# A decoder layer with 64 experts: weights packed and requested by pairs, the last norm's additions on VectorE

## The chip, the cores and the metric

The kernel runs on one core of a Trainium2 chip. The metric is the device time of one execution in microseconds (us). The core's engines are TensorE (PE, its weight loads PEld), VectorE (DVE), ScalarE (ACT), GpSimd (POOL) and SyncE (SP), which here only issues transfers. Each engine works through its own instructions in order and waits on semaphores for the others. Sixteen DMA engines serve every queue.

## The reference

All is float32. `x` has 32 batches of 256 tokens of width 256, the context has 32 batches of 120 tokens. Three stages follow each other, each with a residual and a layer norm:

```python
x = layernorm(x + self_attention(x))          # 16 heads of 16, rotary q and k
x = layernorm(x + cross_attention(x, ctx))    # 16 heads, two softmaxes of 8 dims each, a1 - lam * a2
x = layernorm(x + ffn(x))

# ffn: 64 experts, top 6 of them for each token, at most 96 tokens an expert
scores = sigmoid(x @ router_weight.T)
_, top_idx = top_k(scores + expert_bias, 6)
probs = top_scores / sum(top_scores)
y = gelu(xs @ w1[e]) @ w2[e]                   # xs: the 96 slots of expert e, 256 -> 128 -> 256
out[token] += probs * y
out += gelu(x @ sw1.T) @ sw2.T                 # the shared expert, 256 -> 512 -> 256
```

## The kernel before

**Order of the work.** Every engine is wrapped in `InOrder` (lines 162 to 190): its call is at line 172, so nearly every row of the profile carries L172, and it ties each instruction to the one before it on its engine. So the order in which the Python code calls `pe`, `dve`, `act`, `pool` and `sp` is the order on those engines. Buffers are given out by a scheduler: `tile(..., tag=..., bufs=n)` takes one of n slots of that tag that its readers have left, whichever it is; a name of its own with `bufs=1` takes always the same slot.

**Stage one, the attentions (lines 282 to 1008).** Each batch has a list of steps (lines 398 to 491), written by hand as (tick, part, function). A tick runs, in this order, the parts "pre", the score matmuls of the batches in their score phases together with what reads them (`maxima`: a maximum on VectorE into `pad_mx`; `weights`: an exponential on ScalarE into `pt`), then "av", "mm" and "post". A batch starts 16 ticks after the one before, so several are under way, and ticks that agree modulo 16 run together: tick 62 of one batch with tick 14 and tick -2 of later ones. The steps that matter here:

- `xback(0)` and `xback(1)` (ticks 60 and 61, line 818) turn the cross-attention's result into four PSUM banks of the tag "tr" (four slots in all, `bank()` at line 196). `xweigh(i)` (line 828) reads two of them on VectorE: for each softmax a reciprocal, two products into `rd` and `parts`, and then GpSimd takes the difference into `at`.
- `values` (tick 14, "av", line 743) is the self-attention's product with v. It takes a slot of "tr" too, tile `av`.
- `bias_x` (line 616) adds the output bias to the residual `xt` on GpSimd.
- `store` (line 964) writes the normed tokens to DRAM three times: transposed into `x2T_d`, as the start of the sum `acc[0]`, and zeros into `acc[1]`.
- `dispatch` (line 948) scatters each token's row, with its 64 probabilities and a code of the token (321 numbers), to its experts' places in `slots`.

**The shared expert (`shared`, lines 205 to 276)** is a generator that yields after each piece of TensorE work, 65 pieces: for each block of 512 tokens two pieces `h` (matmuls into a bank of `scp`, then a GELU into `gT`), two pieces for the block before (into a bank "tr", then a copy into `ys`). What a piece leaves for ScalarE (`before`) is called at the start of the next piece. `load` reads a block of `x2T_d` into one of three buffers.

**Stage two, the experts and the last norm (lines 1011 to 1233).** One loop over slots. `n = slot - START` counts pairs of experts: pair n is turned by TensorE (`turn`), pair n-1 does its first product (`up`), n-2 its second (`down`), and `scatter` of pair n-3 weighs the result on VectorE into `ye` and adds it to DRAM with one indirect DMA of GpSimd for each of the two experts, the first to `acc[0]`, the second to `acc[1]`. Weights and rows are requested by SP for groups of four experts: `rows_of`, `expert_weights` (a `w1t` of 512 B rows, a `w2t` of 1 KB rows), three groups ahead, through `fetch_for` in every second slot. `four` has ten buffers of 4 KB per partition, which serve the weights and later the last norm's tiles. In two of three slots up to END a piece of the shared expert is run, after that two in each slot.

From slot END on, each slot has also a step of the last norm for blocks of 512 tokens (class `Last`, lines 1121 to 1168): `fetch` (SP reads the two sums), `add` (GpSimd adds them), `stats` (VectorE adds the result to `ys` and takes mean and variance), `scale` (GpSimd: variance plus epsilon, the power -1/2, the offset in two instructions), `put` (ScalarE normalises four times 256 columns; SP writes `out`). A step calls `add` for block s, `stats` and `scale` for block s-1 and `put` for block s-2.

Of the kernel before, what the change touches and what calls it, by code (L numbers as in the profile page):

```python
# [11 lines left out]
F32 = mybir.dt.float32  # L12
# [24 lines left out]
def tile_decoder_layer(  # L37
# [18 lines left out]
    w1: bass.AP,  # L56
    w2: bass.AP,
# [8 lines left out]
    NT = B * T  # L66
    assert T == 2 * P and S <= P
# [8 lines left out]
    x2T_d = dram.tile([D, NT], F32, name="x2T_d")  # L76
# [123 lines left out]
    TB = min(512, NT)  # L200
# [4 lines left out]
    def shared(ypool):  # L205


        def load(k):
            t = ffn.tile([P, D // P, TB], F32, tag="x2T", name="x2T", bufs=3)
            sp.dma_start(  # L210
                out=t,
                in_=x2T_d[:, k * TB : (k + 1) * TB].rearrange("(c p) t -> p c t", p=P),
            )
            return t
# [17 lines left out]
        loaded = {k: load(k) for k in range(2)}  # L232
        gTs = {}
        for k in range(NBLK + 1):
            for f2 in range(2):
                if k == NBLK:
                    continue
                if f2 == 0 and k + 2 < NBLK:
                    loaded[k + 2] = load(k + 2)
                if before:  # L240
                    before()
                hp = scp.tile([P, 2, 512], F32, tag="sc", name="h")
                for f in range(2):
                    f0 = (2 * f2 + f) * P
                    for c in range(D // P):
                        pe.matmul(
                            hp[:, f, :TB],
                            lhsT=w_s1[:, c, f0 : f0 + P],
                            rhs=loaded[k][:, c, :],
                            start=(c == 0),  # L250
                            stop=(c == D // P - 1),
                        )
                gT = gTs[k, f2] = ffn.tile([P, 2, TB], F32, tag="gT", name="gT", bufs=4)
                before = lambda hp=hp, gT=gT: gelu(hp, gT)
                yield
# [26 lines left out]
    with ExitStack() as one:  # L282
# [101 lines left out]
        class Batch:  # L384
# [13 lines left out]
            def steps(self):  # L398
# [17 lines left out]
                    (-2, "pre", self.bias_x),  # L416
# [49 lines left out]
                    (62, "pre", self.xweigh, 1),  # L466
# [497 lines left out]
            def store(self):  # L964

                cols = slice(self.b * T, (self.b + 1) * T)
                sp.dma_start(
                    out=x2T_d[:, cols].rearrange("(c p) t -> p c t", p=P), in_=self.t["x2T"]
                )
# [41 lines left out]
    with ExitStack() as two:  # L1011

        four = two.enter_context(tc.tile_pool(name="four", bufs=10))
        wk = two.enter_context(tc.tile_pool(name="wk2", bufs=2))
        small = two.enter_context(tc.tile_pool(name="small2", bufs=3))
        ypool = two.enter_context(tc.tile_pool(name="ypool", bufs=NBLK))
        ypools.append(ypool)
        EG = 4
        START = 7

        def rows_of(eg):

            xs = wk.tile([CAP, EG, XPW], F32, tag="xs", name="xs", bufs=4)
            sp.dma_start(
                out=xs,
                in_=slots[eg * EG * CAP : (eg + 1) * EG * CAP, :].rearrange(
                    "(e s) d -> s e d", s=CAP
                ),
            )
            return xs  # L1030

        def tokens_of(eg):

            code = xs_of[eg][:, :, D + NE]
            empty = small.tile([CAP, EG], F32, tag="empty", name="empty")
            dve.tensor_scalar(empty, code, 0.0, slot_f[:CAP, :], ALU.is_equal, ALU.mult)
            token = small.tile([CAP, EG], F32, tag="token", name="token")
            dve.tensor_scalar(token, code, -1.0, float(NT), ALU.mult, ALU.add)
            idx = small.tile([CAP, EG], I32, name=f"idx{eg}", bufs=1)
            dve.tensor_add(idx, token, empty)  # L1040
            return idx

        def expert_weights(eg):
            es = slice(eg * EG, (eg + 1) * EG)
            w1t = four.tile([P, EG, D // P, F], F32, tag="four", name="w1t")
            sp.dma_start(out=w1t, in_=w1[es].rearrange("e (c p) f -> p e c f", p=P))
            w2t = four.tile([P, EG, D], F32, tag="four", name="w2t")
            sp.dma_start(out=w2t, in_=w2[es].rearrange("e p d -> p e d"))
            return w1t, w2t

        class Pair:


            def __init__(self, n):
                self.es = (2 * n, 2 * n + 1)

            def turn(self):
                self.ps = bank()[:, : 4 * CAP].rearrange("p (e c t) -> p e c t", e=2, c=2)
                for k, e in enumerate(self.es):
                    for c in range(D // P):  # L1060
                        pe.transpose(
                            self.ps[:, k, c, :],
                            xs_of[e // EG][:, e % EG, c * P : (c + 1) * P],
# [7 lines left out]
            def up(self):  # L1071
                self.ps = bank()[:, : 2 * CAP].rearrange("p (e t) -> p e t", e=2)
                for k, e in enumerate(self.es):
                    for c in range(D // P):
                        pe.matmul(
                            self.ps[:, k, :],
                            lhsT=weights_of[e // EG][0][:, e % EG, c, :],
# [9 lines left out]
            def down(self):  # L1087
                self.ps = bank()[:CAP].rearrange("p (e d) -> p e d", e=2)
                for k, e in enumerate(self.es):
# [3 lines left out]
                        rhs=weights_of[e // EG][1][:, e % EG, :],  # L1093
# [4 lines left out]
            def scatter(self):  # L1098
                ye = wk.tile([CAP, 2, D], F32, tag="ye", name="ye", bufs=6)
                for k, e in enumerate(self.es):  # L1100
# [3 lines left out]
                        xs_of[e // EG][:, e % EG, D + e : D + e + 1],  # L1104
# [6 lines left out]
                            ap=idx_of[e // EG][:, e % EG : e % EG + 1], axis=0  # L1111
# [9 lines left out]
        class Last:  # L1121
# [4 lines left out]
            def fetch(self):  # L1126
                self.sums = []
                for n in range(2):
                    a = four.tile([P, NQ, D], F32, tag="four", name=f"a{n}")
# [5 lines left out]
            def add(self):  # L1135
                pool.tensor_add(self.sums[0], self.sums[0], self.sums[1])

            def stats(self):
                y = ys[self.k]
                dve.tensor_add(y, y, self.sums[0])  # L1140
# [5 lines left out]

            def scale(self):
                rs = small.tile([P, NQ], F32, tag="rs", name="rs")
                pool.tensor_scalar(rs, self.mv[:, :, 1], LN_EPS, None, ALU.add)
                self.rstd = small.tile([P, NQ], F32, tag="rstd", name="rstd")  # L1150
                pool.tensor_tensor(self.rstd, rs, mhalf[:, :NQ], ALU.pow)
                self.off = small.tile([P, NQ], F32, tag="off", name="off")
                pool.tensor_tensor(self.off, self.mv[:, :, 0], self.rstd, ALU.mult)
                pool.tensor_scalar(self.off, self.off, -1.0, None, ALU.mult)

            def put(self):
                o = four.tile([P, NQ, D], F32, tag="four", name="o")
# [8 lines left out]
                sp.dma_start(  # L1166
# [17 lines left out]
        def fetch_for(eg):  # L1184
            if eg < NE // EG:
                xs_of[eg] = rows_of(eg)
                weights_of[eg] = expert_weights(eg)

        while more or steps < NBLK + 3:
# [8 lines left out]
            if slot == 1:  # L1198
                for eg in range(3):
                    weights_of[eg] = expert_weights(eg)  # L1200
            if slot == START - 2:
                for eg in range(3):
                    xs_of[eg] = rows_of(eg)
            if 0 <= n < NP and n % (EG // 2) == 0:
                eg = n // (EG // 2)
                idx_of[eg] = tokens_of(eg)

            if slot < START or slot < END and n % 3 < 2:
# [3 lines left out]
            if slot >= END and (steps == 0 or steps > NBLK or steps - 1 in whole):  # L1212
                for part, behind in (
                    (Last.add, 0),
                    (Last.stats, 1),
                    (Last.scale, 1),
                    (Last.put, 2),
                ):
                    if part is Last.add:
                        for k in range(0 if steps == 0 else steps + 2, min(steps + 3, NBLK)):  # L1220
                            last[k].fetch()
# [7 lines left out]
            if 0 <= n - 2 < NP:  # L1229
                pairs[n - 2].down()  # L1230
                if n % 2 == 1:
                    fetch_for((n - 2) // 2 + 3)
# [3 lines left out]
def _rotary(seq):  # L1236
# [5 lines left out]
    return [np.repeat(f(angles).astype(np.float32), 2, axis=1) for f in (np.cos, np.sin)]  # L1242

# [46 lines left out]
```

## Time and profile before

| what | us |
|---|---|
| median of 10 runs | 2003.45 |
| lowest and highest of them | 1996.02, 2006.68 |
| the profiled execution | 2004.6 |
| its span, first to last instruction | 2002.9 |

| stage (us from the span's start) | PE busy | DVE busy | ACT busy | POOL busy |
|---|---|---|---|---|
| 200 to 1400, attentions (1200 us) | 1190.9 | 866.2 | 681.8 | 766.3 |
| 1707.2 to 1772, experts (64.8 us) | 64.80 | 19.80 | 20.08 | 21.84 |
| 1772 to 1870.6, experts (98.6 us) | 88.46 | 28.73 | 20.59 | 48.15 |
| 1870.6 to 1914.6, last scatters (44.0 us) | 44.00 | 5.27 | 9.54 | 25.06 |
| 1914.6 to 1926.5 (11.9 us) | 0.43 | 8.00 | 6.95 | 11.18 |
| 1926.5 to 1990.6, last norm (64.1 us) | 64.06 | 38.20 | 42.16 | 60.10 |
| 1990.6 to 2002.9, end (12.3 us) | 0.11 | 3.31 | 8.45 | 2.55 |

A row gives the time in which each engine was busy within that stretch; an engine whose number is near the length of the stretch had hardly a pause in it. The page of the whole execution says 95% for PE, 62% for DVE, 51% for ACT and 59% for POOL, which are means over these stages. The rows that the prediction quotes are of four kinds. A row of waits names the engine and what it did next, who released it, the us in total, how often, and the longest. A row in order of time has the start, the duration, the engine, the instruction with its tiles (output <- inputs), its shapes, and in brackets how long the engine had stood idle and who released it. A row of a window has the stretch, its length, busy us (and instructions) of PE, PEld, DVE, ACT and POOL, the granted TensorE clock, the share of time in which the DMA engines were busy, and GB/s. A row of DMA issues has the tile, the queue, the kind, how many, and the us from issue to landing.

### The profile page before, as it was taken

Reading aid. Unit: us, or ns where it says so; the run is one execution under the profiler, and the core shown is the slowest. Engines: PE = TensorE matmul, PEld = TensorE weight load, DVE = VectorE, ACT = ScalarE, POOL = GpSimd, SP = SyncE. Lnnn points to the kernel's source line nnn. Section 1 sums busy time; section 2 is a strip of 40 time slices with the busy share of each in tenths; the row PEclk is TensorE's granted clock in tenths of the full one; section 3 lists DMA queues with packets and bytes.
Section 4 is the critical chain, followed back from the end, with each engine's and each line's share of the span. In section 5 each row is a group of like instructions: output and inputs, shape, how many; then the busy total and the mean of one; then the engine's idle time right before and its main releaser. Section 6 shows DMA issues by size and latency. Waiting matters only on the chain.

```text
span 2002.9 us, 43322 instructions
## 1 busy us (share of the span) xinstructions
PE 1906.0 (95%) x17800; PEld 1300.8 (65%) x17800; DVE 1244.4 (62%) x2750; ACT 1012.5 (51%) x1445; POOL 1185.5 (59%) x1191
## 2 busy tenths in 40 slices
PE   5999999999999999999999999999999888998977
PEld 3566666666666666666666666666666655776745
DVE  3366777777777777777777777777777643232155
ACT  1345555555555555555555555555555432321356
POOL 6233466666666666666666666666665446244687
PEclk8899999999999999999999999999999979998989
DMA  9100021111111111111111111111100014787495
GB/s 248 48 14 9 30 70 54 47 49 42 35 35 32 33 34 35 34 34 32 31 31 38 32 31 32 32 31 31 32 20 20 17 49 116 184 214 177 62 332 210
DMA packets 131813, 132.06 MB, mean 66 GB/s; under 512 B 32763, under 2 KB 118996, under 8 KB 131616
## 3 DMA queue, kind: packets, MB, share of 16 engines
q1 hardware_dynamic: 103408, 115.22, 18.8%
q0 software_dynamic: 25600, 13.02, 3.9%
q8 instruction: 140, 2.29, 0.4%
q10 hardware_dynamic: 2608, 1.07, 0.2%
q14 instruction: 57, 0.47, 0.1%
HBM read 74.62 MB, written 111.04 MB: 93 GB/s over the span
## 4 chain that ended last, share of the span: by engine, by line
PE 80%; DVE 8%; DMA 6%; POOL 3%; issue 2%; ACT 1%; SPq 0%; DVEq 0%; POOLq 0%; ACTq 0%
PE tr L172 38%; PE sc L172 26%; PE av L172 12%; DMA acc<-ye,idx 5%; PE h L172 3%; DVE pad_mx L172 2%; DVE parts L172 1%; POOL slots L172 1%; ACT pt L172 1%; DVE rd L172 1%; DVE rest L172 1%; DVE count L172 1%; DMA a<-acc 1%; DVE ye L172 0%; DVE sel L172 0%
## 5 line engine op out<-in xcount | busy, mean ns | idle before, releaser
L172 DVE TENSOR_REDUCE pad_mx<-sc 128x4 f32<-128x1024 f32 (+1 forms) x512 | 608.4, 1189 | 376.8 <-PE sc L172 371.4
L172 ACT ACTIVATE pt<-sc 128x1024 f32<-128x1024 f32 (+1 forms) x512 | 523.6, 1024 | 399.2 <-PE sc L172 399.0
L172 PE MATMUL sc<-qT,kT 32*128 32x256 f32 (+1 forms) x4096 | 574.4, 405 | 12.3 <-ACT pt L172 7.8
L172 PE MATMUL sc<-kT,qT 32*128 32x256 f32 (+1 forms) x4096 | 564.1, 396 | 10.6 <-ACT pt L172 5.4
L172 POOL DMA_INDIRECT slots<-xpt,slot x384 | 389.0, 1013 | 95.6 <-issue 92.3
L172 PEld LDWEIGHTS sc<-qT,kT 32*128 32x128 f32 (+1 forms) x4096 | 341.2, 184 | 127.1 <-issue 64.8
L172 PEld LDWEIGHTS sc<-kT,qT 32*128 32x128 f32 x4096 | 349.0, 185 | 94.2 <-issue 24.3
L172 POOL TENSOR_TENSOR qT<-qT,mT 128x512 f32<-128x512 f32 x128 | 163.5, 1295 | 144.5 <-ACT mT L172 144.5
L172 PE MATMUL tr<-w_qkv,xT 128*128 128x256 f32 (+1 forms) x512 | 193.6, 512 | 8.5 <-DMA xT<-in_xT 8.5
L172 POOL TENSOR_SCALAR rs<-mv 128x2 f32<-128x2 f32 (+1 forms) x80 | 30.1, 376 | 240.1 <-DVE mv L172 238.9
L172 POOL DMA_INDIRECT acc<-ye,idx x64 | 90.1, 1408 | 108.2 <-DVE ye L172 57.3
L172 ACT COPY ot<-av 128x512 f32<-128x512 f32 x192 | 112.1, 586 | 81.4 <-PE av L172 81.2
L172 PEld LDWEIGHTS tr<-w_qkv,xT 128*128 128x128 f32 x512 | 90.8, 192 | 77.5 <-issue 72.3
L172 PE MATMUL av<-pt,pad_v 128*32 128x256 f32 x2048 | 126.5, 388 | 10.2 <-DVE parts L172 10.2
L172 PE MATMUL h<-x2T,w_s 128*128 128x512 f32 x256 | 115.7, 602 | 12.2 <-DMA a<-acc 11.5
L172 PE MATMUL av<-pt,pad_xv 120*32 120x256 f32 x2048 | 126.3, 387 | 0.2
L172 POOL TENSOR_TENSOR rc<-qkb,cosr 128x512 f32<-128x512 f32 x64 | 82.5, 1290 | 74.2 <-DVE qkb L172 69.3
L172 PE MATMUL tr<-w_s,gT 128*128 128x256 f32 x512 | 117.1, 387 | 0.8 <-DVE ye L172 0.8
L172 ACT COPY kT<-tr 128x512 f32<-128x512 f32 (+1 forms) x128 | 70.3, 574 | 89.7 <-PE tr L172 89.7
L172 PEld LDWEIGHTS tr<-w_s,gT 128*128 128x128 f32 x512 | 99.6, 195 | 18.9 <-issue 3.8
L172 POOL TENSOR_TENSOR at<-parts 128x256 f32<-128x256 f32 x64 | 46.5, 726 | 108.8 <-DVE parts L172 108.8
L172 POOL TENSOR_TENSOR pad_qk<-rc,qkb 128x256 f32<-128x256 f32 x128 | 104.9, 840 | 5.0
(141 smaller groups left out, 2845.4 us busy)
## 6 DMA issues: line engine op xcount, KB each, us to landing
a<-acc SPq DMA_DIRECT2D x32, 512.0 KB, 5.9
xT<-in_xT SPq DMA_DIRECT2D x32, 256.0 KB, 6.4
xt<-in_x SPq DMA_DIRECT2D x32, 256.0 KB, 2.7
x2T_d<-T SPq DMA_DIRECT2D x32, 256.0 KB, 2.2
acc<-xpt SPq DMA_DIRECT2D x32, 256.0 KB, 2.7
acc<-zero SPq DMA_DIRECT2D x32, 256.0 KB, 3.0
x2T<-x2T_d SPq DMA_DIRECT2D x16, 512.0 KB, 7.8
w1t<-in_w SPq DMA_DIRECT2D x16, 512.0 KB, 6.2
```

The costliest lines, as they stand in the source:

```text
L172: ins = f(*args, **kwargs)
```

## The change

Six things change, in four places of the code.

1. The host packs the two weights of each expert side by side and the experts by pairs (`_pairs_of_experts`), so that one partition's row of a pair is 4 KB. `expert_weights` and `rows_of` request one pair, six pairs ahead, in every slot. The buffers of the weights (`four0` to `four9`), rows (`xs0` to `xs7`) and `ye` are taken in turn by name, each with `bufs=1`. `tokens_of` runs for every pair.
2. `x2T_d` is laid out by blocks, so that a block is read in rows of 4 KB; four buffers in place of three, and the third block is loaded at the start.
3. `xweigh(1)` goes from "pre" to "post" of tick 62, and `bias_x` from "pre" to "post" of tick -2.
4. In the last norm `add` is gone: VectorE adds both sums to `ys`. The epsilon is added on VectorE, the power stays on GpSimd, and the offset is one instruction on VectorE, in the step after. `put` comes one step later, and ScalarE issues the write of `out`. A step calls `offset` for block s-2, `put` for s-3 and `stats` for s-1.
5. Pieces of the shared expert run in three of four slots up to END in place of two of three.
6. `ys` has two buffers fewer.

```diff
@@ load, shared
-            t = ffn.tile([P, D // P, TB], F32, tag="x2T", name="x2T", bufs=3)
-            sp.dma_start(
-                out=t,
-                in_=x2T_d[:, k * TB : (k + 1) * TB].rearrange("(c p) t -> p c t", p=P),
-            )
+            t = ffn.tile([P, D // P, TB], F32, tag="x2T", name="x2T", bufs=4)
+            sp.dma_start(out=t, in_=x2T_d[k])
...
@@ steps
-                    (-2, "pre", self.bias_x),
+                    (-2, "post", self.bias_x),
...
-                    (62, "pre", self.xweigh, 1),
+                    (62, "post", self.xweigh, 1),
...
@@ stage two
-        four = two.enter_context(tc.tile_pool(name="four", bufs=10))
+        four = two.enter_context(tc.tile_pool(name="four", bufs=1))
...
-        EG = 4
+        AHEAD = 6
...
+        def next_four(shape):
+            return four.tile(shape, F32, name=f"four{next(fours) % 10}")
...
-        def expert_weights(eg):
-            es = slice(eg * EG, (eg + 1) * EG)
-            w1t = four.tile([P, EG, D // P, F], F32, tag="four", name="w1t")
-            sp.dma_start(out=w1t, in_=w1[es].rearrange("e (c p) f -> p e c f", p=P))
-            w2t = four.tile([P, EG, D], F32, tag="four", name="w2t")
-            sp.dma_start(out=w2t, in_=w2[es].rearrange("e p d -> p e d"))
-            return w1t, w2t
+        def expert_weights(n):
+            wt = next_four([P, 2, D // P * F + D])
+            sp.dma_start(out=wt, in_=w12[n])
+            return wt
...
-                ye = wk.tile([CAP, 2, D], F32, tag="ye", name="ye", bufs=6)
+                ye = wk.tile([CAP, 2, D], F32, name=f"ye{self.n % 6}", bufs=1)
...
@@ Last
-            def add(self):
-                pool.tensor_add(self.sums[0], self.sums[0], self.sums[1])
-
             def stats(self):
                 y = ys[self.k]
-                dve.tensor_add(y, y, self.sums[0])
+                for a in self.sums:
+                    dve.tensor_add(y, y, a)
...
-            def scale(self):
                 rs = small.tile([P, NQ], F32, tag="rs", name="rs")
-                pool.tensor_scalar(rs, self.mv[:, :, 1], LN_EPS, None, ALU.add)
+                dve.tensor_scalar(rs, mv[:, :, 1], LN_EPS, None, ALU.add)
                 self.rstd = small.tile([P, NQ], F32, tag="rstd", name="rstd")
                 pool.tensor_tensor(self.rstd, rs, mhalf[:, :NQ], ALU.pow)
+
+            def offset(self):
                 self.off = small.tile([P, NQ], F32, tag="off", name="off")
-                pool.tensor_tensor(self.off, self.mv[:, :, 0], self.rstd, ALU.mult)
-                pool.tensor_scalar(self.off, self.off, -1.0, None, ALU.mult)
+                dve.scalar_tensor_tensor(
+                    self.off, self.mv[:, :, 0], -1.0, self.rstd, ALU.mult, ALU.mult
+                )
...
-                sp.dma_start(
+                act.dma_start(
                     out=flat[self.rows, :].rearrange("(p q) d -> p q d", q=NQ), in_=o
                 )
...
@@ the loop
-            if slot < START or slot < END and n % 3 < 2:
+            if slot < START or slot < END and n % 4 < 3:
                 pieces_on(1)
...
+                for part, behind in ((Last.offset, 2), (Last.put, 3), (Last.stats, 1)):
...
+                fetch_for(n - 2 + AHEAD)
```

## The prediction

> **What bounds the kernel now.** I read the windows by stage first, then the waits inside each stage, then the DMA answers and the order of time at the few places where an engine stood still. From 200 to 1400 us the batches of the two attentions overlap and TensorE is busy 198 to 199 us of every 200. One wait stands out there (engine, who released it, us in total, times, longest):
>
> ```profile
> PE av L172 <- DVE parts L172: 9.8, 26, 1.2
> ```
>
> In the order of time one of these waits looks like this (start, duration, engine, what, idle before it):
>
> ```profile
> 621.80 0.42 DVE L172 TENSOR_TENSOR parts<-tr,rd 128x256 f32<-128x256 f32 x1
> 622.38 1.93 PE L172 MATMUL av<-pt,pad_v 128*32 128x256 f32 x32 [0.34 <-DVE parts L172]
> 622.98 1.15 DVE L172 TENSOR_REDUCE pad_mx<-sc 128x8 f32<-128x960 f32 x1
> ```
>
> The weighted sum of the first attention needs a PSUM bank; it gets one that the older batch's `xweigh(1)` has just read. So TensorE stops 0.34 us once in each batch, and the next maximum on VectorE stands behind the same instructions.
>
> The experts' stage begins near 1707. It has windows with the weights' traffic and without (us, busy us of PE, PEld, DVE, ACT, POOL, clock, DMA share, GB/s):
>
> ```profile
> 1676.00:1690.00 14.00, 9.22 (x35) 7.57 (x34) 5.43 (x24) 4.75 (x4) 10.70 (x11) 0.76 1.07 296
> 1753.00:1858.00 105.00, 94.86 (x478) 71.20 (x477) 31.12 (x90) 22.65 (x34) 47.79 (x34) 0.93 0.81 187
> 1858.00:1900.00 42.00, 42.00 (x176) 30.09 (x175) 5.74 (x15) 12.85 (x12) 27.06 (x20) 1.00 0.45 59
> 1908.00:1930.00 22.00, 10.50 (x37) 7.38 (x36) 13.26 (x36) 10.45 (x17) 19.42 (x17) 0.78 0.96 361
> ```
>
> ```profile
> acc<-ye,idx POOLq DMA_INDIRECT x34, 6.6
> ...
> acc<-ye,idx POOLq DMA_INDIRECT x20, 3.4
> ```
>
> The two lines are the scatters of 1753 to 1858 and of 1858 to 1910, with the median us from issue to landing. Each scatter adds to `acc`, so it waits for the one before it on the same half. With weights in flight a pair of experts takes 105/17 = 6.2 us, without them 4.1 (the issues at 1871.36 and 1875.47). TensorE finishes the experts at 1873, but the last scatter lands at E = 1904.6: **the scatters' chain bounds this stage**, not TensorE.
>
> After E the last norm runs:
>
> ```profile
> 1922.50 2.35 POOL L172 TENSOR_TENSOR a<-a,a 128x1024 f32<-128x1024 f32 x1
> 1924.88 1.23 DVE L172 TENSOR_TENSOR y<-y,a 128x1024 f32<-128x1024 f32 x1 [1.91 <-POOL a L172]
> 1924.93 1.26 POOL L172 TENSOR_SCALAR rs<-mv 128x4 f32<-128x4 f32 x1
> 1926.27 1.04 POOL L172 TENSOR_TENSOR rstd<-rs,mhalf 128x4 f32<-128x4 f32 x1
> 1927.88 2.36 POOL L172 TENSOR_TENSOR a<-a,a 128x1024 f32<-128x1024 f32 x1
> 1989.66 0.23 POOL L172 TENSOR_SCALAR rs<-mv 128x4 f32<-128x4 f32 x1
> ```
>
> A step lasts 5.4 us and GpSimd is full in it. The first additions wait 3.7 us after E for `a`, and meanwhile ScalarE stands 20.8 us before the first `o`; the GELUs behind it hold TensorE for 11.5 us. From E to the end of the span it is 2002.9 - 1904.6 = 98.3 us.
>
> **The change part by part.** The sum is made against the span of 2002.9; the profiled run took 2004.6 and the median is 2003.45, so I take the difference from the median.
>
> *A, `xweigh(1)` and `bias_x` after the tick.* The bank for `av` can no longer be the one of `xweigh(1)`, whose reader now comes later in VectorE's order. Free by then is the bank of the query transposes; ScalarE's copy of them ran from 621.05 to 621.63, and the last score matmul ended near 622.03. So the 0.34 us go: 9.8 us over 26 batches. What comes late: VectorE now does its maximum (1.16) first and the last `parts` ends near 625.0 instead of 623.06; `at` and `bias_x` follow on GpSimd (0.73 + 1.27), so its dispatches move from 625.3 to about 627. TensorE transposes `at` two ticks (6 us) after that wait, and GpSimd is free a third of the time: nothing. Bounds: 0, if another wait ends just as late, and -10. I take **-9.8**.
>
> *B, experts' requests.* A pair now brings 0.52 MB of weights in rows of 4 KB and 0.25 MB of rows, right after an older pair's `ye`; before, 1.5 MB came for two pairs. Rows of 4 KB ran at 361 GB/s (1908 to 1930), rows of 512 B and 1 KB at 296 (1676 to 1690): 0.52 x (1/296 - 1/361) = 0.3 us less DMA time per pair. The mixed queue of 1753 to 1858 moved a MB in about 3.7 us, so a burst took 5.6 us and put 2 x (6.2 - 4.1) = 4.2 us onto the scatters. The new one takes about 2.4. If its cost is in proportion, a pair takes 4.1 + 1.8 = 5.9 us; if the first 1.4 us hide under the 1.41 us in which GpSimd issues, as they seem to before, 4.1 + 1.0 = 5.1. TensorE itself needs 2.09 us a pair (starts 1859.87 to 1861.96) and 27 pieces of 3.45 us over 32 pairs instead of 24, so 5.0. Ends are 6.2 (no gain) and 5.0; I take the middle, 5.6, since both rows of landing (3.4 and 6.6) stay in the mix. The weights burden 22 pairs: 22 x 0.6 = **-13**; ends 0 and -24 (TensorE's own end, scatters landed near 1880). The three pieces moved forward fill TensorE's 10.1 us of waits for `ye`. Sixteen more requests on SP (0.3 to 0.5 us each) and 48 more index instructions (0.16 to 0.22 us) lie on queues that are two thirds idle: nothing; with that cover gone, 6 and 9 us.
>
> One rule speaks against B. The Trainium skill, "DMA: Bandwidth & Descriptors", section "Specifications", has 512 B as the smallest transfer at line rate, so packing would bring nothing; its section "Bandwidth" asks for 1 MiB per DMA, so splitting would cost. The trace's 296 against 361 GB/s disagrees with the first. By the rule B would be about 0 and the sum +1, 2004.6.
>
> *C, the last norm.* GpSimd loses the 2.35 us addition, the `rs` and both `off`. VectorE's step: two additions 2 x 1.23 and 0.06 between; four pairs of statistics 2.22 (1920.75 to 1922.97); `rs` 0.2 (0.23 on GpSimd alone). Then the power, which stays on GpSimd: 1.04 plus 0.15 for both handovers. `offset` of that block is the very next instruction on VectorE, so **VectorE waits out the power**, and the next block's additions are queued behind it. `offset` 0.2: in all 6.3 us against 5.4. The end: E + 3.7 for `a`, the second addition and the statistics of block 0, 3.4; 15 x 6.3 = 94.5; `rs`, power, offset 1.7; `put` 2.1; from the last `o` to the end 3.7 as before. Together 109.1, against 98.3: **+11**. Ends: -7, if the wait hides (15 x 1.2 less), and +14, if each step is 6.5.
>
> *D, the rest.* `put` one step later lets two more pieces run before ScalarE blocks: on the new E the 11.5 us stall of TensorE goes. But TensorE would then end near 1875 + 26 x 3.45 = 1965, some 25 us ahead of VectorE's chain, so the gain is not seen. Each `o` now takes the buffer of an `a` of a block two later, and waits for that addition: ScalarE runs at VectorE's pace. The output leaves through ScalarE's queue, 16 x 0.45 us (its issues at the start took 0.33 to 0.8), under that same pace: nothing; were ScalarE the bound, six `put` after TensorE's end are 6 x 2.6 = 16 us and 3 more, to 1984. SP loses 64.0 us of waits for `o`, but the loads behind them were three blocks ahead. `x2T` in 4 KB rows with a fourth buffer loads earlier what nobody waited for. All **0**.
>
> Sum: -9.8 - 13 + 11 = -11.8, so 2003.45 - 11.8 = **1991.6 us**.
>
> **The rivals.** *R1, slower.* VectorE's round through GpSimd's power is the bound of the last 100 us, and the experts' scatters are no faster, because each pair now meets a burst of its own and TensorE another wait in place of `parts`: +11 alone, 2014. It decides as soon as A and B bring less than 11 us together; beyond 0.2% when they bring under 7. For it: 6.3 against 5.4 is read directly; against it: 0.34 us in every batch. *R2, faster than forecast.* The smaller bursts hide and the scatters follow TensorE at 5.0: B = -24, 1980.6; for it, quiet gaps in the DMA rows (26 to 44 GB/s in some slices of 1753 to 1858). *R3, the bank stays.* The allocation still gives `av` the bank of `xweigh(1)`: then TensorE waits for the maximum and `parts`, from 622.05 to about 624.1, 2.1 us x 28 = +59 in place of -9.8: 2060. The order in which banks come free speaks against it. *R4, no difference.* The scatters stay at 6.2 us a pair, since the bytes in front of them are nearly the same (B = 0), and A and C cancel: -9.8 + 11, 2004.7; for it, a landing of 6.6 against 3.4 us, which bytes alone may set.
>
> **How the numbers follow.** About 4 us (0.2%) is what a measurement of this kernel can tell from no change. Forecast (1984 to 1999.4) 0.42; R2 0.20; within 0.2%, mostly R4, 0.14; R1 0.18; R3 0.06. Faster 0.62, same 0.14, slower 0.24. The forecast's own range is 1984 to 1999; the range reaches into R2 and R1, 1976 to 2011.
>
> **What would show it.** Right: TensorE no longer waits for `parts`; pairs of scatters 5.0 to 5.9 us apart with weights in flight; the two `y` additions 6.3 us from block to block, VectorE idle about 1.2 us before each `off`, released by the power; TensorE ending some 20 us before VectorE. Wrong: steps near 5.1 us (C falls to -7 and the time to the 1970s), scatters still 6.2 us a pair, or `av` waiting 2 us.

## The result and the profile after

The changed kernel takes 2023.7 us (median of 13 runs, 2019.85 to 2029.34), the kernel before 2002.0 beside it: a ratio of 1.0113, 95% interval 1.0101 to 1.0125. It is **slower by 1.1%**, some 22 us; the prediction had 12 us faster, and its range ended at 2011. The profiled execution has a span of 2019.1 us, 16.2 more than before.

Four marks tell where these 16.2 us arose: the last store of `x2T` is issued 12.3 us later (1673.9 before, 1686.2 after), the first scatter of the experts another 3.4 later, the time from first to last scatter is 9.3 shorter (177.4, 168.1), and the time from the last scatter to the end 9.8 longer (103.2, 113.0). So the first stage lost what the prediction wanted to gain there.

The waits of TensorE from 200 to 1500 us, after (engine, who released it, us in total, times, longest):

```profile
PE sc L173 <- DVE pad_mx L173: 8.2, 25, 0.4
```

The wait of `av` for `parts` is gone, as foretold. A wait of nearly its size stands in its place: score matmuls now wait for a maximum on VectorE, once in each batch. The order of time around one of them, first VectorE's and then GpSimd's instructions (start, duration, engine, what, idle before it):

```profile
632.20 1.23 DVE L173 TENSOR_REDUCE pad_mx<-sc 128x4 f32<-128x1024 f32 x1 [0.72 <-PE sc L173]
633.34 0.28 DVE L173 TENSOR_REDUCE tot<-sg 128x2 f32<-128x128 f32 x1
633.65 3.22 DVE L173 TENSOR_SCALAR tot<-tot 128x2 f32<-128x2 f32 x1
636.91 0.17 DVE L173 RECIPROCAL tot<-tot 128x2 f32<-128x2 f32 x1
637.11 0.29 DVE L173 TENSOR_TENSOR xpt<-sg,tot 128x128 f32<-128x128 f32 x1
637.32 1.22 DVE L173 TENSOR_REDUCE pad_mx<-sc 128x4 f32<-128x1024 f32 x1
```

```profile
628.72 0.71 POOL L173 TENSOR_TENSOR at<-parts 128x256 f32<-128x256 f32 x1 [4.14 <-DVE parts L173]
629.40 1.26 POOL L173 TENSOR_TENSOR xt<-xt,b_out 128x512 f32<-128x512 f32 x1
630.82 0.99 POOL L173 DMA_INDIRECT slots<-xpt,slot  x1 [0.16 <-issue]
632.12 0.97 POOL L173 DMA_INDIRECT slots<-xpt,slot  x1 [0.30 <-issue]
633.11 1.29 POOL L173 TENSOR_TENSOR x<-x,b_xout 128x512 f32<-128x512 f32 x1
634.34 2.50 POOL L173 TENSOR_TENSOR qT<-qT,mT 128x512 f32<-128x512 f32 x2
```

An addition to 256 numbers takes 3.22 us. It is issued at 633.65, while GpSimd adds `b_xout`, and ends at 636.87, when GpSimd has ended its third addition in a row (634.34 + 2.50 = 636.84). The next maximum starts 5.1 us after the one before it (632.20 to 637.32). The same instructions in the kernel before, VectorE's and then GpSimd's:

```profile
628.89 1.23 DVE L172 TENSOR_REDUCE pad_mx<-sc 128x4 f32<-128x1024 f32 x1 [0.79 <-PE sc L172]
...
630.34 0.17 DVE L172 TENSOR_SCALAR tot<-tot 128x2 f32<-128x2 f32 x1
...
631.65 1.23 DVE L172 TENSOR_REDUCE pad_mx<-sc 128x4 f32<-128x1024 f32 x1 [0.60 <-PE sc L172]
```

```profile
623.16 0.73 POOL L172 TENSOR_TENSOR at<-parts 128x256 f32<-128x256 f32 x1 [2.30 <-DVE parts L172]
623.85 1.27 POOL L172 TENSOR_TENSOR xt<-xt,b_out 128x512 f32<-128x512 f32 x1
...
627.59 1.29 POOL L172 TENSOR_TENSOR x<-x,b_xout 128x512 f32<-128x512 f32 x1
630.75 2.65 POOL L172 TENSOR_TENSOR qT<-qT,mT 128x512 f32<-128x512 f32 x2 [1.88 <-ACT mT L172]
```

There the distance is 2.76 us (628.89 to 631.65): GpSimd stood idle for 1.88 us between `x<-x,b_xout` and `qT<-qT,mT`, and `tot` ran in that gap. The instruction over all batches, before and after (duration in ns min/median/max, first and last start):

```profile
L172 DVE TENSOR_SCALAR tot<-tot x32: 168/169/3793, 239.8 to 1683.1; 128x2 f32<-128x2 f32 x32
```

```profile
L173 DVE TENSOR_SCALAR tot<-tot x32: 168/3222/3340, 239.4 to 1695.4; 128x2 f32<-128x2 f32 x32
```

The order of GpSimd's row is the same in both kernels, with `bias_x` (the `xt` row) behind `at`. What changed is its place in time: `at` waits for a `parts` that comes later, and `bias_x`, both dispatches and what follows come later with it. `x<-x,b_xout` started 1.30 us ahead of the first of the two maxima before and starts 0.91 us behind it now, so that no gap is left. The page's shares by line of the chain that ended last now hold "DVE tot L173 5%", which was not among those of before.

The windows of the experts, after, and the landing of scatters in them (columns as in the prediction):

```profile
1747.00:1850.00 103.00, 103.00 (x556) 78.62 (x555) 37.66 (x127) 25.78 (x38) 50.84 (x37) 1.00 0.82 214
1850.00:1909.00 59.00, 55.19 (x233) 39.21 (x233) 11.47 (x36) 16.60 (x18) 36.66 (x26) 0.97 0.47 74
```

```profile
acc<-ye,idx POOLq DMA_INDIRECT x37, 4.9
...
acc<-ye,idx POOLq DMA_INDIRECT x26, 3.3
```

In this execution the scatters land after 4.9 us with weights in flight (6.6 before) and TensorE has no idle time. The experiments show that it was the best of eight.

The last norm, one step on VectorE and its neighbours:

```profile
1994.49 2.48 DVE L173 TENSOR_TENSOR y<-y,four 128x1024 f32<-128x1024 f32 x2
...
1999.26 0.17 DVE L173 TENSOR_SCALAR rs<-mv 128x4 f32<-128x4 f32 x1
1999.60 1.01 POOL L173 TENSOR_TENSOR rstd<-rs,mhalf 128x4 f32<-128x4 f32 x1 [5.22 <-DVE rs L173]
2000.64 0.16 DVE L173 SCALAR_TENSOR_TENSOR off<-mv,rstd 128x4 f32<-128x4 f32 x1 [1.21 <-POOL rstd L173]
2000.72 2.48 DVE L173 TENSOR_TENSOR y<-y,four 128x1024 f32<-128x1024 f32 x2
2000.84 2.08 ACT L173 ACTIVATE four<-y,off,rstd 128x256 f32<-128x256 f32 x4 [2.81 <-DVE off L173]
```

From `y` to `y` it is 6.23 us; VectorE waits 1.21 us for the power before `off`, and ScalarE waits for VectorE. This is as foretold. TensorE ended at 1985.9, 33 us before the end.

### The profile page after: what moved, and what is told of

Read it like the earlier page. It is cut to its first block, busy times and chain, and to the rows that moved or that the text cites. A ratio compares the mean times of both kernels' runs of the same rounds, so it can differ in the third digit from the quotient of the medians.

```text
span 2019.1 us, 43371 instructions
## 1 busy us (share of the span) xinstructions
PE 1916.0 (95%) x17800; PEld 1297.3 (64%) x17800; DVE 1371.2 (68%) x2846; ACT 1014.5 (50%) x1445; POOL 1116.6 (55%) x1127
## 4 chain that ended last, share of the span: by engine, by line
PE 75%; DVE 13%; POOL 4%; DMA 3%; issue 3%; ACT 1%; DVEq 0%; POOLq 0%; SPq 0%; ACTq 0%
PE tr L173 35%; PE sc L173 26%; PE av L173 12%; DVE tot L173 5%; DVE pad_mx L173 4%; PE h L173 2%; DMA acc<-ye,idx 2%; DVE y L173 2%; POOL slots L173 1%; DVE st L173 1%; POOL rstd L173 1%; DMA four<-acc 1%; ACT pt L173 1%; DVE mv L173 1%; POOL pad_qk L173 0%
## 5 line engine op out<-in xcount | busy, mean ns | idle before, releaser
L173 DVE TENSOR_REDUCE pad_mx<-sc 128x4 f32<-128x1024 f32 (+1 forms) x512 | 608.6, 1190 | 326.2 <-PE sc L173 319.4
L173 ACT ACTIVATE pt<-sc 128x1024 f32<-128x1024 f32 (+1 forms) x512 | 523.8, 1025 | 413.5 <-PE sc L173 413.3
L173 PE MATMUL sc<-qT,kT 32*128 32x256 f32 (+1 forms) x4096 | 580.2, 406 | 13.0 <-ACT pt L173 7.8
L173 PE MATMUL sc<-kT,qT 32*128 32x256 f32 (+1 forms) x4096 | 562.2, 395 | 18.2 <-DVE pad_mx L173 12.2
L173 POOL DMA_INDIRECT slots<-xpt,slot x384 | 388.3, 1011 | 95.6 <-issue 94.3
L173 PEld LDWEIGHTS sc<-qT,kT 32*128 32x128 f32 (+1 forms) x4096 | 338.3, 183 | 127.8 <-issue 61.5
L173 PEld LDWEIGHTS sc<-kT,qT 32*128 32x128 f32 x4096 | 347.8, 184 | 112.8 <-DVE pad_mx L173 31.2
L173 POOL TENSOR_TENSOR qT<-qT,mT 128x512 f32<-128x512 f32 x128 | 159.5, 1268 | 89.4 <-ACT mT L173 89.4
L173 PE MATMUL tr<-w_qkv,xT 128*128 128x256 f32 (+1 forms) x512 | 193.6, 512 | 8.5 <-DMA xT<-in_xT 8.5
L173 POOL TENSOR_SCALAR rs<-mv 128x2 f32<-128x2 f32 x64 | 14.0, 218 | 255.9 <-DVE mv L173 255.9
L173 ACT COPY ot<-av 128x512 f32<-128x512 f32 x192 | 112.3, 585 | 78.4 <-PE av L173 78.3
L173 POOL DMA_INDIRECT acc<-ye,idx x64 | 90.5, 1413 | 102.0 <-DMA acc<-ye,idx 46.1
L173 PEld LDWEIGHTS tr<-w_qkv,xT 128*128 128x128 f32 x512 | 90.8, 192 | 77.5 <-issue 63.8
L173 POOL TENSOR_TENSOR at<-parts 128x256 f32<-128x256 f32 x64 | 46.3, 723 | 162.5 <-DVE parts L173 162.4
L173 PE MATMUL av<-pt,pad_xv 120*32 120x256 f32 x2048 | 126.8, 389 | 0.1
L173 PE MATMUL av<-pt,pad_v 128*32 128x256 f32 x2048 | 126.5, 389 | 0.0
L173 POOL TENSOR_TENSOR rc<-qkb,cosr 128x512 f32<-128x512 f32 x64 | 82.5, 1289 | 74.2 <-DVE qkb L173 69.3
L173 PE MATMUL h<-x2T,w_s 128*128 128x512 f32 x256 | 117.5, 607 | 5.5 <-ACT gT L173 5.5
L173 PE MATMUL tr<-w_s,gT 128*128 128x256 f32 x512 | 117.3, 387 | 3.8 <-DVE ye L173 3.8
L173 ACT COPY kT<-tr 128x512 f32<-128x512 f32 (+1 forms) x128 | 70.3, 574 | 88.4 <-PE tr L173 88.4
L173 POOL TENSOR_TENSOR rstd<-rs,mhalf 128x2 f32<-128x2 f32 (+1 forms) x80 | 62.3, 778 | 94.7 <-DVE rs L173 89.4
L173 PEld LDWEIGHTS tr<-w_s,gT 128*128 128x128 f32 x512 | 99.5, 195 | 21.4 <-DVE ye L173 4.2
```

Of the source, the lines that this page charges most:

```text
L173: ins = f(*args, **kwargs)
```

## The experiments

Each ratio below is against the kernel before, run on the same chip beside it. Kernels that were not measured beside each other are compared by subtracting these ratios; 0.001 is 2 us. The expectations give the distance of two batches ("pitch") in the steady middle of the first stage, 48.81 us before and 49.40 after; the texts below give the mean over all 31 distances between stores of `x2T`, which is smaller because the last batches follow closer.

**1. Both steps back.** The changed kernel with

```diff
-                    (-2, "post", self.bias_x),
+                    (-2, "pre", self.bias_x),
...
-                    (62, "post", self.xweigh, 1),
+                    (62, "pre", self.xweigh, 1),
```

> The changed kernel with xweigh(1) and bias_x back ahead of the tick, all else as changed. Theory T1 (the move lets GpSimd's three long additions run back to back just as VectorE issues route(4)'s 128x2 addition, which is then held 3.2 us): the batch pitch goes from 49.40 back to 48.81 us, the last x2T store from 1686 to about 1674, and the 3.5 us at the start of the experts may stay; time 2007 to 2012. Rival T2 (the 12 us come from other edits that reach into the first stage): pitch stays 49.4, time within 3 us of 2023.7. TensorE waits for parts again, 0.3 us a batch, under both.

Measured: 2013.6 us, ratio 1.0049 (1.0027 to 1.0071), so 13 us less than the changed kernel and 1.6 above the range that T1 gave. The stores of `x2T` are again 47.43 us apart (from the first issue to the last, over 31), as before the change; after it they are 47.82. The pitch in the steady part is 48.81 us, as T1 had it. T1 stands, T2 falls. What remains, 10 us over before, must lie in the other parts.

**2. Only `bias_x` back** (the first of the two edits above).

> The changed kernel with bias_x alone back ahead of the tick; xweigh(1) stays behind it. If T1 is right and the 1.27 us of bias_x make the GpSimd chain reach VectorE's tot: tot takes 0.17 us in most batches, no av wait, pitch 48.81 less 0.3 = 48.5 to 48.8, time 2001 to 2010. If xweigh(1) alone is enough to bring GpSimd's additions onto tot: pitch stays 49.2 to 49.5, time 2018 to 2024.

Measured: 1995.8 us, ratio 0.9962 (0.9940 to 0.9984): 30 us less than the changed kernel, faster than before and below the range expected. `tot` has a median of 169 ns, TensorE waits for nothing between 200 and 1500 us, and the stores come 46.99 us apart (48.41 in the steady part). So `xweigh(1)` moved alone gains more than the prediction gave both moves, and `bias_x` behind the tick costs 0.83 us a batch.

**3. `bias_x` later still.**

```diff
-                    (-2, "post", self.bias_x),
+                    (2, "post", self.bias_x),
```

> The changed kernel with bias_x still later, behind tick 2, where GpSimd has nothing else to do for some 5 us. If the loss was the meeting of GpSimd's row of additions with tot and not the lateness of bias_x: tot 0.17 us, stores 47.0 us apart, time about 28 below the changed kernel, as with bias_x back in its place. If a later bias_x costs by itself: within 5 us of the changed kernel or above it.

Measured: 1997.4 us, ratio 0.9969 (0.9953 to 0.9985), stores 46.92 us apart. In the order of time, VectorE and then GpSimd of this kernel:

```profile
622.85 0.17 DVE L173 TENSOR_SCALAR tot<-tot 128x2 f32<-128x2 f32 x1
```

```profile
621.08 1.29 POOL L173 TENSOR_TENSOR x<-x,b_xout 128x512 f32<-128x512 f32 x1
623.26 2.65 POOL L173 TENSOR_TENSOR qT<-qT,mT 128x512 f32<-128x512 f32 x2 [0.88 <-ACT mT L173]
...
632.21 1.25 POOL L173 TENSOR_TENSOR xt<-xt,b_out 128x512 f32<-128x512 f32 x1
```

`bias_x` (the `xt` row) now runs 14 us after `at`, where it ran 0.7 after it, and costs nothing. GpSimd's gap from 622.37 to 623.26 is back, and `tot` runs in it. Lateness was harmless; the meeting with `tot` was the price.

**4. Without the held instruction.** The guard against a sum of zero is left out:

```diff
                     dve.tensor_reduce(tot, sg, AX.X, ALU.add)
-                    dve.tensor_scalar(tot, tot, 1e-20, None, ALU.add)
                     dve.reciprocal(tot, tot)
```

> The changed kernel without the addition of 1e-20 to tot in route(4) (one 128x2 instruction of 0.17 us a batch by its own price; the quotient's guard against a sum of zero is left out). If that instruction is the one held: the pitch falls to 48.5 to 48.9 us and the time by 12 to 20, to 2004 to 2012, far more than 28 x 0.17 = 5 us. If VectorE is held by GpSimd whatever it issues there: the reciprocal or the next maximum takes the 3 us in its place, pitch 49.3 to 49.4, time 2019 to 2024.

Measured: 2010.3 us, ratio 1.0034 (1.0014 to 1.0055), 16 us less than the changed kernel. The time is that of the first theory, but its reason is only half right:

```profile
625.69 0.28 DVE L173 TENSOR_REDUCE tot<-sg 128x2 f32<-128x128 f32 x1
626.00 0.17 DVE L173 RECIPROCAL tot<-tot 128x2 f32<-128x2 f32 x1
626.20 3.15 DVE L173 TENSOR_TENSOR xpt<-sg,tot 128x128 f32<-128x128 f32 x1
629.27 1.21 DVE L173 TENSOR_REDUCE pad_mx<-sc 128x4 f32<-128x1024 f32 x1
```

```profile
625.47 1.29 POOL L173 TENSOR_TENSOR x<-x,b_xout 128x512 f32<-128x512 f32 x1
626.70 2.49 POOL L173 TENSOR_TENSOR qT<-qT,mT 128x512 f32<-128x512 f32 x2
```

The hold passes to the next instruction of a certain kind. The sum and the reciprocal ran at full speed under GpSimd's additions (0.28 and 0.17 us); the product of two tiles in SBUF (`xpt<-sg,tot`, median 3151 ns instead of 293) was held until GpSimd's row ended. What was won is the work that no longer follows the hold: the reciprocal now lies inside GpSimd's row, and the product itself was what waited, so the maximum comes 4.7 us after the one before it (624.55 to 629.27) in place of 5.1. The stores are 47.46 us apart, about half way between 47.82 and 46.99; in the steady part it is 49.00 us, a little above the 48.5 to 48.9 expected.

These rows fit what the Trainium skill, "SBUF — State Buffer", section "Who interferes with whom", states: VectorE shares one pair of SBUF ports with GpSimd, the first to issue has it for its whole instruction and the other is blocked. By that section a `tensor_scalar` can need the shared pair, a `tensor_tensor` with both inputs in SBUF contends with a GpSimd instruction that reads SBUF, and a `tensor_reduce` does not contend. The runs agree with each kind that they show: 3.22 and 3.15 us for the first two, 0.28 for the third. In length they differ from it: the page speaks of one instruction, and here the hold lasted from the first of three GpSimd additions to the end of the third. The port itself no profile shows.

**5 and 6. The moves on the kernel before:** both, and `xweigh(1)` alone.

> The kernel before with the two moved steps alone (xweigh(1) and bias_x behind the tick), nothing of the experts or the norm. Theory T1 (the moves together cost the whole of the first stage's loss): the x2T stores 47.8 us apart in place of 47.43, tot 3.2 us long in most batches, time 10 to 16 above before. The prediction on record had 10 below before. Rival (the loss needs the new stores of x2T as well): pitch 47.4, time within 3 us of before.

> The kernel before with xweigh(1) alone behind the tick. If this move by itself does what the prediction said of both: no wait of TensorE for parts, stores 47.0 us apart, time 10 to 18 below before. If it needs the other edits: within 4 us of before.

Measured: both moves 2016.1 us, ratio 1.0082 (1.0059 to 1.0105), `tot` 3225 ns in the median, stores 47.87 us apart; `xweigh(1)` alone 1988.1 us, ratio 0.9936 (0.9916 to 0.9957), stores 47.01 us apart. 16 us slower, a little over the range expected, and 13 us faster. The experts, the norm and the layout of `x2T` are not needed for either.

**7. `offset` behind `stats`.** The changed kernel with

```diff
-                for part, behind in ((Last.offset, 2), (Last.put, 3), (Last.stats, 1)):
+                for part, behind in ((Last.put, 3), (Last.stats, 1), (Last.offset, 2)):
```

> The changed kernel, in each step of the last norm offset behind stats instead of ahead of put, so that the power on GpSimd runs under the next block's additions and statistics. Theory (VectorE waits out the power, 1.2 us a step, and VectorE's round bounds the end): step 6.2 to about 5.0 us, 16 x 1.2 = 19 us off VectorE's chain; something else ends a little later than that, TensorE or ScalarE at 1990 to 2002 by its own rows, so the time falls by 12 to 19, to 2005 to 2012. Rival (ScalarE's put or the buffers in turn set the step): step stays above 5.9, time within 4 us of 2023.7.

Measured: 2007.5 us, ratio 1.0016 (0.9999 to 1.0032), 19 us less than the changed kernel. From the last scatter to the end it is 97.2 us in place of 113.0. The step:

```profile
1950.69 2.48 DVE L173 TENSOR_TENSOR y<-y,four 128x1024 f32<-128x1024 f32 x2
...
1955.47 0.17 DVE L173 TENSOR_SCALAR rs<-mv 128x4 f32<-128x4 f32 x1
1955.55 0.16 DVE L173 SCALAR_TENSOR_TENSOR off<-mv,rstd 128x4 f32<-128x4 f32 x1
1955.62 2.48 DVE L173 TENSOR_TENSOR y<-y,four 128x1024 f32<-128x1024 f32 x2
```

```profile
1955.81 1.90 POOL L173 TENSOR_TENSOR rstd<-rs,mhalf 128x4 f32<-128x4 f32 x1 [3.03 <-DVE off L173]
```

4.93 us from `y` to `y`, with no wait. The power now runs beside the two additions and takes 1.90 us where it took 1.01, but a whole step is there to hide it.

**8. Both repairs:** `bias_x` back and `offset` behind `stats`, and **9.** the same with the pieces as before (`n % 3 < 2`).

> The changed kernel with bias_x back ahead of the tick and offset behind stats in the step of the last norm. If the two gains add (each alone brought about 28 and 19 us against the changed kernel of the same measurement): 1976 to 1984 on the scale of a kernel before at 2004. If the end of TensorE, which follows the experts, takes over: 1984 to 1992.

> As the kernel with bias_x back and offset behind stats, but with a piece of the shared expert in two slots of three, as before, in place of three of four. If the pieces put the first scatter 3.4 us later (11.0 in place of 7.6 us after the first copy of a pair's rows) and the chain of scatters sets the rest: first scatter 7.6 us after that copy, the last one 3 to 4 us earlier, time 3 to 4 lower. If TensorE sets the end: the three pieces come back behind the experts at 3.45 us each, time 0 to 7 higher.

Measured: number 8 takes 1978.3 us, ratio **0.9887** (0.9868 to 0.9907), 23 us faster than before; the two gains, 30 and 19 us alone, come to 45 together. Number 9 takes 1987.3, ratio 0.9933 (0.9914 to 0.9953), 9 us more than number 8, a little over the 0 to 7 expected. The first scatter did come 7.6 us after the first copy instead of 11, but the whole became longer: once VectorE's wait is gone, TensorE's last pieces set the end, and three of them came back behind the experts. TensorE ends 6.9 us later in its profile (1968.4, 1961.5), and from the last scatter to the end it is 104.2 us in place of 96.8. In number 8 TensorE ends at 1961.5, and the last 19 us are ScalarE's six `put`, the bound that the prediction put in its part D for that case.

**10. Few weights.** The changed kernel with

```diff
                 xs_of[n] = rows_of(n)
-                weights_of[n] = expert_weights(n)
+                weights_of[n] = weights_of[n - AHEAD]
```

> The changed kernel without the weights of pairs 6 to 31: each uses again those of the pair six before it, so 13.6 MB less are moved in the experts' stage, and the result of these pairs is not the experts'. The rows and scatters stay. Theory B1 (the time in which a scatter's bytes share the queues with weights sets the pace of scatters, whatever the size of rows or requests): pairs p5 to p21 fall from about 6.0 to 4.1 to 5.0 us, first to last scatter from about 173 to 135 to 155, time 15 to 30 below the changed kernel. Rival B2 (pace set by TensorE, pieces included, or by GpSimd): 5.7 or more a pair, time within 8 us of the changed kernel.

Measured: 1999.0 us, ratio 0.9971 (0.9960 to 0.9981), 28 us less than the changed kernel. Pairs p5 to p21 follow each other after 4.81 us, first to last scatter takes 147.2 us, and a scatter lands after 3.7 us where it took 4.9 in the same window of the changed kernel. The rival falls: neither TensorE nor GpSimd set the pace, the traffic of the weights did, and it costs this stage 21 to 30 us against the 168 to 177 of the kernels with all weights.

**11. Unpacked weights.** Two requests for each pair in place of one, w1 in rows of 512 B and w2 of 1 KB (the matmuls that read them follow suit):

```diff
-            wt = next_four([P, 2, D // P * F + D])
-            sp.dma_start(out=wt, in_=w12[n])
-            return wt
+            es = slice(2 * n, 2 * n + 2)
+            wt = next_four([P, 2, 2, D])
+            w1t = wt[:, 0].rearrange("p e (c f) -> p e c f", c=D // P)
+            sp.dma_start(out=w1t, in_=w1[es].rearrange("e (c p) f -> p e c f", p=P))
+            sp.dma_start(out=wt[:, 1], in_=w2[es].rearrange("e p d -> p e d"))
+            return w1t, wt[:, 1]
```

> The changed kernel with the weights unpacked: two requests a pair, w1 in rows of 512 B and w2 in rows of 1 KB, as before the change, everything else as changed. By the prediction (rows of 4 KB take 0.3 us less a pair, doubled where two scatters wait): pace p5 to p21 0.3 to 0.6 us slower, time 6 to 12 above the changed kernel. Theory B1 (bytes alone): pace and time the same, within 4 us.

Measured: 2017.2 us, ratio 1.0069 (1.0043 to 1.0094). It was expected 6 to 12 above the changed kernel, or level; it stands 9 below. Its profile differs little from that of the changed kernel: pairs p5 to p21 follow each other after 5.79 us (5.74), first to last scatter takes 168.9 us (168.1). As the 9 us may be the occasion of the measurement rather than the edit, the same edit was made to number 8 and measured beside number 8 itself, on one chip (a slower one, where the kernel before took 2056.2):

> The kernel with bias_x back and offset behind stats, with the weights unpacked in two requests a pair (w1 in rows of 512 B, w2 in rows of 1 KB). If packing brings what the prediction gave it: 6 to 12 above the packed one beside it on the same chip. If packing brings nothing: within 4 us of it. If two smaller requests are better than one of 512 KB: 4 to 8 below it.

> The kernel with bias_x back and offset behind stats once more, beside the unpacked one: 0.987 to 0.991 of before, pace of pairs p5 to p21 5.8 to 6.2 us.

Measured: unpacked 2039.0 us, ratio 0.9913 (0.9887 to 0.9939), packed 2036.9, ratio 0.9907 (0.9876 to 0.9937); pace 6.14 and 6.10 us a pair. The packing into rows of 4 KB brings nothing that can be measured. The intervals are 5 to 6 us each way, so this pair alone does not exclude the 6 us at the low end of what the prediction gave it; run 11, which came out below the packed kernel, speaks against it too.

On this chip number 8 has `tot` at 1.05 us in the median (0.17 on the other) and 49.06 us between batches in the steady part (48.41 on the other). Its rows, GpSimd's and then VectorE's:

```profile
631.96 2.50 POOL L173 TENSOR_TENSOR qT<-qT,mT 128x512 f32<-128x512 f32 x2 [0.45 <-ACT mT L173]
```

```profile
632.19 1.06 DVE L173 TENSOR_SCALAR tot<-tot 128x2 f32<-128x2 f32 x1
...
633.49 1.12 DVE L173 TENSOR_TENSOR xpt<-sg,tot 128x128 f32<-128x128 f32 x1
```

`tot` was issued during the first of the two `qT` additions (1.25 us each) and ended with that one, although the second followed without a gap; `xpt<-sg,tot` then waited out the second. Here the hold lasted for one instruction, as the page has it, and not for the row. Why it lasted for three instructions in the changed kernel and for one here, no run shows.

**12. The experts' part alone.** The changed kernel with the two steps back and the class `Last`, its order and its stores by SP as before (the edit restores what point 4 of the change replaced).

> The changed kernel with the two moved steps back ahead of the tick and the whole last norm as before (first addition, rs and both off on GpSimd, put two steps behind, stores by SP): what is left of the change is the experts' packing, requests and pieces and the layout of x2T. By the prediction: 13 below before. If the experts' part brings nothing, as the time of the kernel with only the two steps back says (10 above before, with a last norm that costs 10): within 4 us of before.

Measured: 1999.9 us, ratio 0.9974 (0.9948 to 1.0000): between the two expectations, nearer to nothing. It has 15 us less than number 1, from which only the last norm and its stores differ; 10 of them stand in that part of the two profiles (112.7 and 102.4 us from the last scatter on).

## Why the prediction was wrong

Several kernels share each part of the code, so each part can be read in several profiles. Us, without those of the slower chip; a row leaves out kernels that have the part in another form:

| | as before | as changed | repaired |
|---|---|---|---|
| stores of `x2T` apart | 47.43, 47.43, 47.24 | 47.82, 47.87, 47.87, 47.79, 47.87 | 46.99, 47.01, 46.99, 46.88, 46.92 |
| pace of pairs p5 to p21 | 6.33, 6.34, 6.31 | 5.74, 6.22, 6.06, 5.83, 6.22, 6.16, 6.08, 5.85 | |
| last scatter to the end | 103.2, 102.9, 103.5, 102.4 | 113.0, 112.7, 112.9, 112.9, 112.8, 112.8, 112.6 | 97.2, 96.8 |

**A was the step that failed: -9.8 predicted, +12 to +16 measured.** Its first half was right and even small: `xweigh(1)` behind the tick frees the bank, the wait for `parts` goes, and the stage gains 13 us (runs 2 and 6). Its second half, the shift of `at` and `bias_x` on GpSimd, was priced in one sentence, "TensorE transposes `at` two ticks (6 us) after that wait, and GpSimd is free a third of the time: nothing", with no loss among its bounds. The prediction had the shift itself, "its dispatches move from 625.3 to about 627", 1.7 us; against VectorE's maximum 2.2 were measured. The chain from `at` to TensorE was indeed no trouble. But a free third of the time is a mean over the stage, and the place was not looked at: behind `bias_x` stood two dispatches, `x<-x,b_xout` and two `qT<-qT,mT`, with one gap of 1.88 us, in which VectorE's `tot` ran. Filling that gap costs 0.83 us a batch, 31 times, 26 us. Runs 2 and 3 show it from both sides: `bias_x` one place earlier or 13 us later, and the loss is gone. No rival named it. R1, the slower one, came nearest: it had another wait of TensorE in place of `parts`, but put A at no gain, not at a loss.

**B was mis-sized: -13 predicted, about -2 by the profiles, -5 with an interval from 0 to -10 by run 12.** The pace was to be 5.6 us; its mean over the eight profiles is 6.02, against 6.33. That is 0.3 us over 16 pairs, or 5 us, and the first scatter gives 3.4 back, since a third piece stands ahead of it (11 us after the first copy instead of 7.6). The profiled execution of the changed kernel, with 5.74, is the best of the eight. The chain of scatters as the bound and traffic as its price hold (run 10). Two terms of its sum were too large. One is the term for the rows: 361 against 296 GB/s came from two windows with different traffic (weights, `x2T` and dispatches in the one, the two sums, `out` and `x2T` without any weights in the other), and was taken for the effect of row length. The other is the 1.4 us of each burst that were to hide under GpSimd's issues: without them the prediction's own sum gave 5.9 us a pair, and 6.02 were measured; no run tests this term by itself. The rule that the prediction had weighed against the packing, of the Trainium skill, "DMA: Bandwidth & Descriptors", section "Specifications", that 512 B is enough for line rate, agrees with run 11: 2039.0 against 2036.9 us. Its other rule, on the size of a DMA, the change did not put to the test: a request for weights had 512 KB before and has 512 KB after.

What the remaining 0.3 us a pair come from is not settled: not from the packing (run 11), nor from the pieces, as run 9 has 5.98 with the pieces as before; that leaves the requests pair by pair, the buffers taken in turn and the layout of `x2T`, which no run changed alone. In the 115 us from the first scatter on, VectorE waits 36 to 38 us for a scatter to leave a `ye` in the three kernels with the experts as before, 4 to 8 in the three of the eight with a pace under 5.9, and 18 to 23 in the other five. Whether these waits are the cause of the pace or follow from it, no run shows.

**C was right: +11 predicted, 10 measured from the last scatter on, 15 by the times of runs 1 and 12.** VectorE waits out the power, the step is 6.2 us where 6.3 was worked out, and run 7 takes the wait away. From the landing of the last scatter (1911.3) to the end it is 107.8 us, worked out as 109.1.

**D was right as far as it was tried.** TensorE ended 27 us ahead of VectorE's last instruction (1985.9, 2013.3; 20 to 25 were expected). That the extra pieces bring nothing there is argued from this lead, no run takes them out of the changed kernel; with the wait gone (run 8 against 9) they bring 9 us. What D says of ScalarE's queue and of `x2T` in rows of 4 KB no run changed alone.

The terms as measured, +12 to +16, -2 to -5 and +10 to +15, hold the 22 us that were measured.

## What to carry to other kernels

An instruction moved on an engine is priced at the place where it lands: list what runs right before and behind it on that engine and what the neighbours issue in the gap that it fills; a share of free time says nothing of it. Where VectorE and GpSimd both work in SBUF, a row of GpSimd's long additions without a gap can hold a tiny VectorE instruction for up to the row's whole length (3.22 us here, 1.06 where it was let in after one of them), so keep gaps where VectorE's short steps fall, or move the long ones to a quiet place. An instruction that waits for another engine's result goes last in the step, behind work that does not need it: that one line was worth 19 us.

## What was not expected of the hardware

- A 128x2 addition on VectorE lasted 3.22 us beside three GpSimd additions in a row, against 0.17 in GpSimd's gap; on the slower chip, beside two in a row, it lasted 1.06. A reduction and a reciprocal beside such additions kept their 0.28 and 0.17 us.
- GpSimd was slowed too: the power on 128x4, 1.01 us while VectorE waits for it, took 1.90 us beside VectorE's additions of 128x1024.
- TensorE's busy time hides much of a wait. In two stretches of 200 us, changed kernel and number 8:

```profile
200.00:400.00 200.00, 199.02 (x2096) 134.69 (x2095) 155.55 (x309) 112.50 (x163) 116.01 (x119) 1.00 0.15 48
```

```profile
200.00:400.00 200.00, 200.00 (x2141) 134.87 (x2139) 150.20 (x311) 114.48 (x165) 121.20 (x123) 1.00 0.17 55
```

  Busy time differs by 1 us, the matmuls recorded by 45 of 2141, 2.1%, which would be 4 us of the 200; from 600 to 800 and from 1000 to 1200 the counts stand 61 and 59 apart, while the whole executions have 17800 each. The waits listed for TensorE, 8.2 us, are less than a third of the 26 us that the meeting costs.
